# Turning the layer-0 feed-forward's quads and the layer-1 attention's pairs by block transposes and two row transfers in place of TensorE transposes

## Chip, cores and metric

One NeuronCore of a Trainium2 chip runs the whole program. The metric is the device time of one execution in microseconds (us), the median of several runs. All data are 32-bit floats.

## What is computed

A two-layer vision tower over 32 images of 3 x 256 x 256. Each image becomes 256 tokens of 256 features. The reference, cut to the order of the work and to the two places that the change touches:

```python
h = tokenizer(x)                                   # 32 x 256 x 256
h = h + L0_attn(layernorm(h))                      # gated attention, relu squared
h = h + L0_ffn(layernorm(h))
h = h + L1_attn(layernorm(h))
h = h + L1_ffn(layernorm(h))                       # experts in 4 heads

# L0_ffn: the 127 best of the 256 tokens of an image go through the layer, the others get x alone
weights = x @ wr + br
sel = x[top 127 tokens by weights]
y = (gelu(sel @ w1 + b1) @ w2 + b2) * weights[sel]
out = zeros.at[sel].set(y) + x

# L1_attn: phases from two small networks, a causal memory over the tokens
key   = tanh(gelu(x @ Wk1 + bk1) @ Wk2 + bk2) * freq * pi
query = tanh(gelu(x @ Wq1 + bq1) @ Wq2 + bq2) * freq * pi
retrieved = real(sum(cumsum(exp(i key) * (x @ Wv + bv)) * exp(-i query))) / sqrt(position * K)
out = x + layernorm(retrieved) @ Wo + bo
```

Here `x` is the layer-normed input of each layer. `sel @ w1` and `x @ Wk1`, `x @ Wq1` sum over features, so on TensorE the features of `sel` and `x` must lie along the partitions; they are made with tokens along the partitions. Turning them round is what the change is about.

## The kernel before, in words

The program is written as five stages. A (tokenizer), B (layer-0 attention), C (layer-0 feed-forward), D (layer-1 attention) are recorded by hand: each engine executes its instructions in the order in which the Python code issues them, and waits are put in where data or buffers need them. E (layer-1 feed-forward) is ordered by a table. The images' states `H[b]` (128 partitions x 2 x 256, token `c * 128 + p` in partition `p`) stay on the chip throughout. All matmuls are recorded at line 116, in the helper `mm`; PSUM has eight banks, taken in turn (`bank`).

**Turning tokens to features** is done in two ways. On TensorE, `transposed` (L180 to 190) and `turn_c` (L225 to 231) transpose 128x128 tiles against an identity into two PSUM banks, and `copy_split` (L192 to 196) copies the first bank by ScalarE (L194), the second by VectorE (L196). Stage B has another way for 14 of its 16 pairs: `blocks_b` (L262 to 271) transposes 32x32 blocks on VectorE into `b_blocks`, and four DMAs write them to a DRAM buffer, `turned_b` (L273 to 277) reads them back by four more DMAs. All DMAs named here are issued by SyncE's queue (SP) in order; SP waits at an issue until what it needs is there.

**Stage B** handles a pair of images a step, t from 0 to 17. In each step it also normalises the following pair (`norm_b`, `blocks_b`). From t = 4 on it ranks the tokens of finished images for stage C: `rank_c` scatters an image's tokens to the DRAM buffer `ranked` by their rank, and `first_ranks` (L220 to 223) loads the first 128 ranks of four images, a quad, into `cs`. At t = 17 `turn_c` turns quad 0, between `gated_b` and `output_b`.

**Stage C** has eight quads, four steps to a quad. `ORDER_C` (L877) says what runs at which step of quad u (step 0 is t = 4u): hidden_c at 0 and 1 (`sel @ w1`, two halves of 16 matmul records each), made at 2 and 3 (`@ w2`, two images each, results written to DRAM by SP at L850), `turn_c` at -1, first_ranks at -8, fetch at 4 and 5 (gathers by GpSimd), update at 5 and 6 (VectorE: `H` updated at L869 and its statistics at L124). In a step the entries are issued in the order of the list, so `turn_c` of the next quad stands between the two `made`. At t = 30, the last but one, `norm_d` normalises the first two pairs of stage D into `cx`.

**Stage D** has 16 pairs of images, three steps of t to a pair. For pair u, `do(k, f)` runs f at t = 3u + k:

- 0: norm_d (L809 to 822) writes the pair's normalised tokens `dx` (four buffers, two per pair)
- 1: turn (L911 to 913), the transposes into `dxT`; residual_d on GpSimd
- 2: hidden, two networks of two 128-wide parts each, and Gelu on ScalarE
- 3: phases: small matmuls, Tanh, then L943, L946, L947 on VectorE, then Sin on ScalarE into `dz`
- 4: match: matmuls of `dz` with itself; VectorE multiplies by the causal mask into `dat` (L963)
- 5: memory: matmuls of `dat` and `dx`, copied to `dm` by ScalarE (L976)
- 6: output: matmuls of `dm` and `wvo` into four banks, statistics by VectorE (L987, L988)
- 7: add_output adds the four banks to `H` (L997) and so frees them; stats_e

Steps of different pairs with the same t are interleaved: at t = 3u + 2 stand hidden of pair u and memory of pair u - 1, at t = 3u + 3 phases of u, output of u - 1 and norm_d of u + 1, at t = 3u + 4 the transposes of u + 1, add_output of u - 1 and match of u. The first pairs differ: pair 1 is turned at t = 2. At t = 6, 9 and 12 the last entries of `ORDER_C` follow, fetches and updates of the last quad.

Of the kernel before, what the change touches and what calls it, by code (L numbers as in the profile page):

```python
# [80 lines left out]
def vit_tower(tc, a, out):  # L81
# [15 lines left out]
    def bank():  # L97
        return ppool.tile([P, 512], F32, name="bank", tag="bank")
# [81 lines left out]
    def transposed(xT, xs, copy):  # L180
# [3 lines left out]
        for k in range(2):  # L184
# [4 lines left out]
                    nc.tensor.transpose(p[:, o : o + P], x[:, c, k * P : (k + 1) * P], ident)  # L189
            copy(k, xT[:, k, :], p[:, 0:w])  # L190

    def copy_split(k, o, i):  # L192
        if k == 0:
            nc.scalar.copy(o, i)  # L194
        else:
            nc.vector.tensor_copy(o, i)  # L196
# [25 lines left out]
        for j in range(4):  # L222
            nc.sync.dma_start(s.x[:, j, :], ranked[b0 + j][0:P, :])

    def turn_c(b0, s, _):  # L225
        s.xsel = p0.tile([P, 2, 4 * P], F32, name="xsel")
        for k in range(2):
            p = bank()
            for j in range(4):
                nc.tensor.transpose(p[:, j * P : (j + 1) * P], s.x[:, j, k * P : (k + 1) * P], ident)  # L230
            copy_split(k, s.xsel[:, k, :], p)

    wpool = region.enter_context(tc.tile_pool(name="w_c", bufs=1))
    region_b = ExitStack()
# [26 lines left out]

    def blocks_b(b0, s):  # L262
        s.d = pdram.tile([32, 16 * NC, 4, 32], F32, name="b_turned", bufs=2)
        y = px.tile([P, 8, 2 * NC, 32], F32, name="b_blocks", bufs=1)
        for j, x in enumerate(s.xs):
            nc.vector.transpose(
                y[:, :, j * NC : (j + 1) * NC, :].rearrange("p f c t -> p c f t"),
                x.rearrange("p c (f t) -> p c f t", t=32),
            )
        for i in range(4):  # L270
            nc.sync.dma_start(s.d[:, :, i, :], y[32 * i : 32 * i + 32].rearrange("p f c t -> p (f c) t"))
# [150 lines left out]
    with (  # L422
# [96 lines left out]
        for t in range(B // 2 + 2):  # L519
            new, old, older, next_one = pair(t) if t else None, pair(t - 1), pair(t - 2), pair(t + 1)  # L520
            next_one = next_one if t else None
            if t == 1:
                turn_b(*new, p2, "bxT")
            if t >= 4:
                turned = turn_weights(2 * (t - 4))
            if old:
                scores_b(*old)
            if new:
                base_b(*new, p2.tile([P, 2 * N], F32, name="base"))
            if t >= 4:  # L530
                ranks(2 * (t - 4), turned)
                if t in (5, 7):
                    first_ranks(2 * t - 10, quads[t // 2 - 2], 0)
            if new:
                queries_b(*new, p2.tile([P, 2 * N], F32, name="bq"), p2.tile([P, 2 * N], F32, name="bk"))
            if old:
                gates_b(*old)
            if t == 1:
                factors_b(*powers)
            if next_one:  # L540
                norm_b(*next_one)
                blocks_b(*next_one)
            if old and t >= 3:
                norms_c(2 * (t - 3))
            if old:
                values_b(*old)
            if next_one:
                bias_b(*next_one)
            if old and t >= 3:
                residuals_c(2 * (t - 3))  # L550
            if next_one:
                turned_b(*next_one, p2, "bxT")
            if older:
                gated_b(*older)
                if t == B // 2 + 1:
                    turn_c(0, quads[0], 0)
                    norms_c(2 * (t - 3))
                    residuals_c(2 * (t - 3))
                output_b(*older)
# [249 lines left out]
    def norm_d(b0, s, pool, name, bufs):  # L809
        s.xs = []  # L810
        for j in range(2):
# [10 lines left out]
                )  # L822
            s.xs.append(x)

    def residual_d(b0, s):
        for j in range(2):
            h = H[b0 + j]
            nc.gpsimd.tensor_tensor(h, h, s.xs[j], ALU.add)
            nc.gpsimd.tensor_tensor(h, h, over(add_row, [P, NC, D], 1), ALU.add)

    with region_c:
        st_d = new_stats("d")

        def hidden_c(b0, s, half):
            if half == 0:
                s.hT = p2.tile([P, 8, 4 * P], F32, name="hT")
            for m in range(4 * half, 4 * half + 4):
                p = bank()
                for k in range(2):
                    mm(p, w1[:, k, m * P : (m + 1) * P], s.xsel[:, k, :], k == 0, k == 1)  # L840
                nc.scalar.activation(s.hT[:, m, :], p, AF.Gelu_apprx_tanh, bias=col("b1", m))

        def made(b0, s, half):
            for j in range(2 * half, 2 * half + 2):
                p = bank()
                for m in range(8):
                    mm(p[:, 0:D], s.hT[:, m, j * P : (j + 1) * P], w2[:, m, :], m == 0, m == 7)
                y = p2.tile([P, D], F32, name="cy", bufs=4)
                nc.vector.tensor_tensor(y, p[:, 0:D], row_c("b2"), ALU.add)
                nc.sync.dma_start(results[b0 + j][:], y)  # L850

        def fetch(b0, s, half):
            s.y = s.y if half else []
            for b in range(b0 + 2 * half, b0 + 2 * half + 2):
                y = px.tile([P, NC, D], F32, name="cx", bufs=8)
                for c in range(NC):
                    k = b * NC + c
                    nc.gpsimd.indirect_dma_start(
                        y[:, c, :], None, results[b][:], bass.IndirectOffsetOnAxis(rank_of[:, k : k + 1], 0)
                    )  # L860
                s.y.append(y)

        def update(b0, s, half):
            for j in range(2 * half, 2 * half + 2):
                b = b0 + j
                st, rs, i = at(st_d, b)
                for c in range(NC):
                    k = b * NC + c
                    nc.vector.scalar_tensor_tensor(  # L869
                        H[b][:, c, :], s.y[j][:, c, :], w_kept[:, k : k + 1], H[b][:, c, :], ALU.mult, ALU.add  # L870
                    )
                    stats(st, i, c, H[b][:, c, :])
            pow_rstd_of(st_d, b0 + 2 * half, 2)

        ORDER_C = ((0, hidden_c, 0), (1, hidden_c, 1), (2, made, 0), (-1, turn_c, 0), (-8, first_ranks, 0),  # L877
                   (3, made, 1), (4, fetch, 0), (5, fetch, 1), (5, update, 0), (6, update, 1))

        def step_c(t):  # L880
            for at_step, do, j in ORDER_C:
                u, r = divmod(t - at_step, 4)
                if r == 0 and 0 <= u < B // 4 and (u > 1 or do is not first_ranks):
                    do(4 * u, quads[u], j)

        END_C = 4 * (B // 4 - 1) + 4
        pairs = [Pair() for _ in range(B // 2)]
        preparing = prepare()
        for t in range(END_C):
            if t == 0:  # L890
                norms_c(B - 2)
                residuals_c(B - 2)
            if t == END_C - 2:
                for u in range(2):
                    norm_d(2 * u, pairs[u], px, "cx", 8)
            step_c(t)
            if t < 2:
                ranks(B - 4 + 2 * t, turn_weights(B - 4 + 2 * t))
            if t >= 8:
                next(preparing, None)  # L900
        passing.close()
# [5 lines left out]
    with (  # L907
        tc.tile_pool(name="d_2", bufs=2, reuse_waits="tile") as p2,
        tc.tile_pool(name="d_8", bufs=8, reuse_waits="tile") as p8,
    ):  # L910
        def turn(b0, s):  # L911
            s.xT = p2.tile([P, 2, 2 * N], F32, name="dxT")
            transposed(s.xT, s.xs, copy_split)

        def hidden(b0, s, i, ms=(0, 1)):

# [3 lines left out]
            for m in ms:  # L920
                p = bank()
                for k in range(2):
                    mm(p, (wk1, wq1)[i][:, k, m * P : (m + 1) * P], s.xT[:, k, :], k == 0, k == 1)
                nc.scalar.activation(g[:, m, :], p, AF.Gelu, bias=bias_d[:, 2 * i + m : 2 * i + m + 1])

        def phases(b0, s):
# [81 lines left out]
        for t in range(3 * (NP - 1) + 8):  # L1008
# [3 lines left out]
                    which(2 * u, pairs[u], *more)  # L1012

            last = t == 3 * NP + 1
            if t != 4:
                do(1, turn)
            if not last:
                do(7, add_output)
            if t != 4:
# [7 lines left out]
            do(2, hidden, 0)  # L1027
            if t == 2:
                do(2, hidden, 1)
                turn(2, pairs[1])  # L1030
            elif t == 5:
                do(2, hidden, 1, (0,))
                match(0, pairs[0])
# [4 lines left out]
            do(3, phases)  # L1038
            if t == 5:
                residual_d(2, pairs[1])  # L1040
            if t > 3:
                do(0, norm_d, p8, "dx", 4)
            if t == 3 * NP:
                output(B - 4, pairs[NP - 2], (0, 1, 2))
            else:
# [740 lines left out]
def _layout(i):  # L1786


    def blocks(w, p=P):
        k, m = w.shape[0] // p, w.shape[1]  # L1790
        return w.reshape(k, p, m).transpose(1, 0, 2)

    def column(v, p=P):
        return v.reshape(-1, p).T

# [29 lines left out]
    def pairs(w):  # L1825
# [12 lines left out]
        "rows_e": np.concatenate([rows_e[n] for n in ROWS_E]),  # L1838
        "wuv": blocks(i["L0_attn_W_uv"]),
        "wo": blocks(i["L0_attn_W_o"]),  # L1840
        "w1": blocks(i["L0_ffn_w1"]),
        "w2": blocks(i["L0_ffn_w2"]),
        "before": before,
        "wk1": blocks(i["L1_attn_Wk1"]),
        "wq1": blocks(i["L1_attn_Wq1"]),
        "wk2": blocks(twice(i["L1_attn_Wk2"])),
        "wq2": blocks(twice(i["L1_attn_Wq2"])),
        "wv1": blocks(i["L1_attn_Wv"]),
# [40 lines left out]
```

## Time and profile before

| what | us |
|---|---|
| median of three runs | 1913.17 (1910.04 to 1913.69) |
| the profiled execution's own time | 1911.49 |
| its span | 1909.7 |
| TensorE busy | 1864.9 |
| VectorE busy | 1313.2 |
| ScalarE busy | 805.8 |
| GpSimd busy | 757.6 |

In the profile, PE is TensorE, PEld its weight loads, DVE VectorE, ACT ScalarE, POOL GpSimd, SP SyncE; L is a line of the kernel. The page gives each engine's busy time and share, then 40 equal slices of the span (digits are tenths), then DMA queues, then the chain: from the last instruction back, at each step to what released it, as shares of the span. A timeline row is start, length, engine, line, operation, tiles written <- read, shapes, count, and in brackets the idle time before it with what ended it. Durations of matmuls overlap, since they are pipelined: one 128x512 record lasts 592 ns, but the next starts 0.43 us after it. PEclk is the share of full speed that the clock of TensorE was granted; in this execution it was 1.00 nearly everywhere, 0.94 and 0.98 in the stretches from 180 and 200 us, 0.84 in that from 1000 us, and lower at the very end. A DMA row gives the number of issues, the size of each and the median time from issue to landing. In the page's list of DMA issues cs<-ranked has 3.5 us for 128 KB.

Stage C's first hidden matmul is at 681.7 us and its last matmul before D's transposes ends at 918 us; D's first transposes are at 917.96 and stage E's work begins at about 1260 us.

### The profile page before, as it was taken

The numbers are of one execution on the slowest core, as the hardware profiler recorded it, in microseconds if no ns is written. First come the engines' busy times: TensorE is split into PE (matmuls) and PEld (weight loads), VectorE is DVE, ScalarE is ACT, GpSimd is POOL, SyncE is SP. The second block draws the span as 40 slices with busy tenths as digits, with TensorE's granted clock in tenths as the row PEclk, the third lists the DMA queues.
The fourth block names the chain that finished last, engine by engine and source line by source line (L and its number), as shares of the span: only waits on it lengthen the run. The fifth ranks groups of instructions, "written<-read, shape, count | busy, mean of one in ns | idle before, by whom it ended". The sixth has DMA issues, their size and how long they took to land.

```text
span 1909.7 us, 36912 instructions
## 1 busy us (share of the span) xinstructions
PE 1864.9 (98%) x14740; PEld 1323.7 (69%) x14740; DVE 1313.2 (69%) x3271; ACT 805.8 (42%) x1632; POOL 757.6 (40%) x792
## 2 busy tenths in 40 slices
PE   9999999999999999999989999999999999999993
PEld 8887566666676776766645555567888878787872
DVE  2335478787878563534465555544999999999998
ACT  0001222121212112122334444447787888888772
POOL 1224233333434253424343433324454545555553
PEclk9999999999999999999999999999999999999995
DMA  9550121212121042212000000001222222222211
GB/s 312 151 156 18 35 61 46 71 42 58 47 54 44 34 136 63 82 54 61 15 20 1 1 1 0 1 18 24 58 52 62 58 57 63 52 63 53 64 44 57
DMA packets 132226, 109.17 MB, mean 57 GB/s; under 512 B 67792, under 2 KB 110288, under 8 KB 131664
## 3 DMA queue, kind: packets, MB, share of 16 engines
q1 hardware_dynamic: 125328, 89.17, 17.4%
q0 software_dynamic: 6144, 16.79, 2.8%
q8 instruction: 118, 1.93, 0.4%
q10 hardware_dynamic: 576, 0.79, 0.1%
q14 instruction: 60, 0.49, 0.1%
HBM read 53.75 MB, written 28.31 MB: 43 GB/s over the span
## 4 chain that ended last, share of the span: by engine, by line
PE 94%; DVE 4%; issue 1%; ACT 0%; DMA 0%; SPq 0%; POOL 0%; DVEq 0%; ACTq 0%
PE bank L116 91%; PE bank L792 2%; PE bank L189 1%; PE bank L230 0%; PE bank L500 0%; DVE six L124 0%; DVE fout L1387 0%; DVE fout L1401 0%; DVE eo L1265 0%; DMA b_turned<-b_blocks 0%; DVE ranges L1288 0%; DVE six L987 0%; DVE fout L1390 0%; DMA bxT<-b_turned 0%; DVE h L869 0%
## 5 line engine op out<-in xcount | busy, mean ns | idle before, releaser
L1184 POOL TENSOR_SCALAR_AFFINE_SELECT et<-et 128x512 f32<-128x512 f32 (+1 forms) x192 | 166.2, 878 | 201.6 <-ACT et L1175 199.7
L1175 ACT ACTIVATE et<-bank 128x512 f32<-128x512 f32 x384 | 207.7, 630 | 30.7 <-PE bank L116 30.2
L116 PE MATMUL bank<-ev,et 128*64 128x68 f32 (+1 forms) x6144 | 198.9, 225 | 0.0
L116 PEld LDWEIGHTS bank<-ev,et 128*64 128x64 f32 x6144 | 191.5, 137 | 5.7 <-issue 4.7
L116 PE MATMUL bank<-g,sx 64*128 64x512 f32 (+1 forms) x512 | 177.6, 486 | 0.0
L116 PE MATMUL bank<-g,sw 64*128 64x512 f32 (+1 forms) x512 | 177.2, 486 | 0.0
L116 PE MATMUL bank<-tokW,patch 128*128 128x256 f32 x768 | 167.6, 381 | 0.0
L116 PEld LDWEIGHTS bank<-tokW,patch 128*128 128x128 f32 x768 | 146.6, 191 | 21.4 <-DMA tokW<-in_tokW_dram 0.7
L116 PE MATMUL bank<-bxT,w_wuv 128*128 128x512 f32 x300 | 133.0, 598 | 2.5 <-DMA bxT<-b_turned 2.5
L1204 ACT COPY eo<-bank 128x280 f32<-128x280 f32 x256 | 96.0, 396 | 68.3 <-PE bank L116 61.6
L116 PEld LDWEIGHTS bank<-g,sx 64*128 64x128 f32 x512 | 93.1, 187 | 31.6 <-issue 22.7
L116 PE MATMUL bank<-wvo,dm 128*128 128x512 f32 x256 | 114.3, 599 | 0.0
L116 PE MATMUL bank<-attn,bv 128*128 128x256 f32 x512 | 113.1, 379 | 0.0
L116 PE MATMUL bank<-w_wo,gT 128*128 128x256 f32 x512 | 113.1, 379 | 0.0
L116 PE MATMUL bank<-w_w,hT 128*128 128x256 f32 x512 | 113.1, 379 | 0.0
L116 PE MATMUL bank<-xsel,w_w 128*128 128x512 f32 x256 | 111.4, 593 | 0.0
L116 PEld LDWEIGHTS bank<-attn,bv 128*128 128x128 f32 x512 | 97.2, 190 | 19.6 <-issue 7.2
L124 DVE BATCH_NORM_STATS2 six<-h 128x6 f32<-128x256 f32 x256 | 105.5, 412 | 4.4
L116 PEld LDWEIGHTS bank<-w_w,hT 128*128 128x128 f32 x512 | 96.6, 190 | 15.3 <-issue 2.9
L116 PEld LDWEIGHTS bank<-g,sw 64*128 64x128 f32 x512 | 93.1, 187 | 20.1 <-issue 9.9
L116 PEld LDWEIGHTS bank<-w_wo,gT 128*128 128x128 f32 x512 | 97.2, 190 | 13.2
L116 PE MATMUL bank<-w_wuv,bxT 128*128 128x512 f32 x240 | 105.4, 592 | 0.0
(276 smaller groups left out, 3712.6 us busy)
## 6 DMA issues: line engine op xcount, KB each, us to landing
patch<-in_patches_dram SPq DMA_DIRECT2D x31, 768.0 KB, 4.6
sw<-sx SPq DMA_DIRECT2D x64, 128.0 KB, 2.3
out_dram<-fout SPq DMA_DIRECT2D x32, 256.0 KB, 2.4
both<-fxT SPq DMA_DIRECT2D x62, 128.0 KB, 2.4
both<-hx SPq DMA_DIRECT2D x62, 128.0 KB, 2.3
b_turned<-b_blocks SPq DMA_DIRECT2D x56, 128.0 KB, 3.3
bxT<-b_turned SPq DMA_DIRECT2D x56, 128.0 KB, 3.1
cs<-ranked SPq DMA_DIRECT2D x32, 128.0 KB, 3.5
```

What stands on the lines that cost most here:

```text
L116: nc.tensor.matmul(o, lhsT, rhs, start=first, stop=last)
L124: nc.vector.bn_stats(six, x)
L189: nc.tensor.transpose(p[:, o : o + P], x[:, c, k * P : (k + 1) * P], ident)
L792: nc.tensor.transpose(p[:, o : o + P], x[:, c, k * P : (k + 1) * P], ident)
L1175: nc.scalar.activation(t2[:, i, :], p, AF.Exp)
L1184: nc.gpsimd.affine_select(out=own, in_=own, pattern=[[0, 2 * n_e], [1, P]], compare_op=ALU.is_ge, fill=0.0, base=0, channel_multiplier=-1,)
L1204: nc.scalar.copy(im.o[:, g * OC : (g + 1) * OC], p[:, 0:OC])
```

## The change

Quads of C and pairs of D are turned as stage B's pairs were, but by larger transfers: VectorE transposes 32x32 blocks (one instruction for a quad, two for a pair), one DMA writes the result to DRAM in rows of 4 KB, one DMA reads it back in pieces of 1 KB. The features come back in another order, four groups of 32 partitions interleaved, so `w1`, `wk1`, `wq1` are laid out by the host in that order (`turned`), and hidden's moving operand `s.f[:, k]` is read with three dimensions, in runs of 32 elements. The transposes at TensorE and the copies that followed them are gone from C and D; pairs 0 and 1 of B keep theirs.

The placing: in C `blocks_c` runs at step -3 and `moved_c`, the read, at step -2, where `turn_c` was at -1. Quad 0 is done at t = 15 of B. For D's pairs 0 and 1 the blocks and the write stand at t = 30 of C, behind norm_d, into free `cs` buffers; the reads are issued at t = 1 and 2 of D. For pairs from 2 on, norm_d moves from step 0 to step -1, and the blocks, write and read follow it there. `blocks` in B and C is one shared buffer; `dxB` in D is one buffer; the DRAM buffer `c_turned` has two.

```diff
+    def blocks_turned(y, xs, d):
+        y5 = y.rearrange("p (f s t) -> p s f t", f=4, t=32)
+        n = 8 // len(xs)
+        for j, x in enumerate(xs):
+            nc.vector.transpose(
+                y5[:, j * n : (j + 1) * n], x.rearrange("p c (k f t) -> p (c k) f t", k=2, f=4)
+            )
+        nc.sync.dma_start(d.rearrange("i q x -> (i q) x"), y)
+
+    def moved(xT, d):
+        nc.sync.dma_start(xT, d.rearrange("i q (f x) -> (q f) i x", f=4))
+        return xT.rearrange("p i (s k t) -> p k s i t", k=2, t=32)
...
-    def turn_c(b0, s, _):
-        s.xsel = p0.tile([P, 2, 4 * P], F32, name="xsel")
...
+    def blocks_c(b0, s, _):
+        s.d = pdram.tile([4, 32, 4 * N], F32, name="c_turned", bufs=2)
+        blocks_turned(px.tile([P, 4 * N], F32, name="blocks", bufs=1), [s.x], s.d)
+
+    def moved_c(b0, s, _):
+        s.f = moved(p0.tile([P, 4, 2 * P], F32, name="xsel"), s.d)
...
+            if t == B // 2 - 1:
+                blocks_c(0, quads[0], 0)
+                moved_c(0, quads[0], 0)
             if older:
                 gated_b(*older)
                 if t == B // 2 + 1:
-                    turn_c(0, quads[0], 0)
...
+    def blocks_d(b0, s, pool, name, shape, bufs):
+        y = pool.tile(shape, F32, name=name, bufs=bufs)
+        s.d = pdram.tile([4, 32, 4 * N], F32, name="c_turned", bufs=2)
+        blocks_turned(y.rearrange("p j d -> p (j d)"), s.xs, s.d)
...
-                    mm(p, w1[:, k, m * P : (m + 1) * P], s.xsel[:, k, :], k == 0, k == 1)
+                    mm(p, w1[:, k, m * P : (m + 1) * P], s.f[:, k], k == 0, k == 1)
...
-        ORDER_C = ((0, hidden_c, 0), (1, hidden_c, 1), (2, made, 0), (-1, turn_c, 0), (-8, first_ranks, 0),
+        ORDER_C = ((0, hidden_c, 0), (1, hidden_c, 1), (2, made, 0), (-3, blocks_c, 0), (-2, moved_c, 0), (-8, first_ranks, 0),
...
             if t == END_C - 2:
                 for u in range(2):
                     norm_d(2 * u, pairs[u], px, "cx", 8)
+                for u in range(2):
+                    blocks_d(2 * u, pairs[u], p0, "cs", [P, 4, D], 2)
...
-        def turn(b0, s):
-            s.xT = p2.tile([P, 2, 2 * N], F32, name="dxT")
-            transposed(s.xT, s.xs, copy_split)
+        def moved_d(b0, s):
+            s.f = moved(p2.tile([P, 4, N], F32, name="dxT"), s.d)
...
-                    mm(p, (wk1, wq1)[i][:, k, m * P : (m + 1) * P], s.xT[:, k, :], k == 0, k == 1)
+                    mm(p, (wk1, wq1)[i][:, k, m * P : (m + 1) * P], s.f[:, k], k == 0, k == 1)
...
-            if t != 4:
-                do(1, turn)
+            if t == 1:
+                do(1, moved_d)
...
             if t == 2:
                 do(2, hidden, 1)
-                turn(2, pairs[1])
+                moved_d(2, pairs[1])
...
-            if t > 3:
-                do(0, norm_d, p8, "dx", 4)
+            if t > 4:
+                do(-1, norm_d, p8, "dx", 4)
+                do(-1, blocks_d, p8, "dxB", [P, 2 * NC, D], 1)
+                do(-1, moved_d)
...
+    def turned(w):
+        w = blocks(w)
+        return w.reshape(4, 32, *w.shape[1:]).swapaxes(0, 1).reshape(w.shape)
...
-        "w1": blocks(i["L0_ffn_w1"]),
+        "w1": turned(i["L0_ffn_w1"]),
...
-        "wk1": blocks(i["L1_attn_Wk1"]),
-        "wq1": blocks(i["L1_attn_Wq1"]),
+        "wk1": turned(i["L1_attn_Wk1"]),
+        "wq1": turned(i["L1_attn_Wq1"]),
```

More of the change, by code (lines that the diff above doesn't have):

```diff
@@ L223, in first_ranks @@
             nc.sync.dma_start(s.x[:, j, :], ranked[b0 + j][0:P, :])
-    def turn_c(b0, s, _):
-        s.xsel = p0.tile([P, 2, 4 * P], F32, name="xsel")
[L227 to L231, printed above, removed]
+    def blocks_c(b0, s, _):
[3 more added lines that the diff above has]
+        s.f = moved(p0.tile([P, 4, 2 * P], F32, name="xsel"), s.d)
     wpool = region.enter_context(tc.tile_pool(name="w_c", bufs=1))
@@ L263, in blocks_b @@
         s.d = pdram.tile([32, 16 * NC, 4, 32], F32, name="b_turned", bufs=2)
-        y = px.tile([P, 8, 2 * NC, 32], F32, name="b_blocks", bufs=1)
+        y = px.tile([P, 4 * N], F32, name="blocks", bufs=1)
+        y = y.rearrange("p (f c t) -> p f c t", f=8, t=32)
         for j, x in enumerate(s.xs):
```

## The prediction, made before the changed kernel ran

> **What bounds the kernel now.** I read the page first: engines, slices, chain.
>
> ```profile
> PE 1864.9 (98%) x14740; PEld 1323.7 (69%) x14740; DVE 1313.2 (69%) x3271; ACT 805.8 (42%) x1632; POOL 757.6 (40%) x792
> ...
> PE   9999999999999999999989999999999999999993
> ...
> PE 94%; DVE 4%; issue 1%; ACT 0%; DMA 0%; SPq 0%; POOL 0%; DVEq 0%; ACTq 0%
> ```
>
> TensorE is the bound almost everywhere: 94% of the chain is matmuls. So a matmul taken away is worth its place in TensorE's queue, if nothing else then comes late. Two stages are touched: layer-0 feed-forward (C, about 675 to 918 us) and layer-1 attention (D, about 919 to 1260 us). Of D I read the timeline of one pair (start, length, engine, line, tiles):
>
> ```profile
> 1105.14 1.04 PE L189 MATMUL bank<-ident,dx 128*128 128x128 f32 x8
> ...
> 1106.11 1.58 PE L116 MATMUL bank<-dz 64*128 64x256 f32 x16
> ...
> 1107.62 3.70 PE L116 MATMUL bank<-dxT,w_wk 128*128 128x512 f32 x8
> ...
> 1114.59 2.78 PE L116 MATMUL bank<-dat,dx 128*128 128x256 f32 x16
> ...
> 1117.40 0.58 ACT L976 COPY dm<-bank 128x512 f32<-128x512 f32 x1 [0.72 <-PE bank L116]
> ```
>
> Each group begins where the one before ends: the pair's transposes, match, hidden, memory, then phases and output. The transposes recur at 1084.14, 1105.14, 1126.15: a pair takes 21.0 us. Two pairs take longer (23.7 and 26.9 us, from 970.5, 994.2 and 1021.1). There TensorE waits:
>
> ```profile
> 975.83 0.66 DVE L196 COPY dxT<-bank 128x512 f32<-128x512 f32 x1
> ...
> 976.54 2.84 PE L116 MATMUL bank<-dxT,w_wk 128*128 128x512 f32 x6 [2.44 <-DVE dxT L196]
> ```
>
> ```profile
> 1000.45 5.49 PE L116 MATMUL bank<-dxT,w_wk 128*128 128x512 f32 x6 [2.64 <-DVE dxT L196]
> ```
>
> VectorE is busy with the last images' updates (L869, L124), and its half of the transpose's copy stands behind them. After the second wait the matmuls run at half speed: the clock granted in 1000 to 1020 us was 0.84, 3.2 us lost. The two waits and the dip are the 2.7 + 5.9 us by which these periods exceed 21.0.
>
> **Removed.** 64 transposes at L230 (8 quads) and 128 at L189 (16 pairs; 16 of L189's 144 belong to B and stay). Their row says 273 ns each, and the Trainium skill ("TensorE: Matmul & The Clock Gate", Part 4: PE-mode transpose) has about 275 ns in a kernel's context; by that 192 of them are 52 us. But the durations overlap: in the timeline eight start at 1105.14 and the next group at 1106.11, 0.97 us; in C eight start at 703.17 and the next matmul at 704.04, 0.87 us. I take the starts: C 8 x 0.87 = 7.0 us, D 0.97 us for each pair but pair 0 (below), 15 x 0.97 = 14.6 us. Also removed: the copies (ACT 585 ns, DVE 658 to 680 ns per quad or pair), off the path except in the two waits.
>
> The two waits go: hidden then needs a transfer made a period before, and not the late VectorE copy. What is late next: hidden's third group takes a PSUM bank that add_output (L997) frees, after the same updates. In the 994 us pair the updates cannot end before about 999.2 (output's last matmuls end at 994.2, one bn_stats, 4.2 us of updates), add_output frees a bank at 999.65; hidden, begun at 995.7, reaches that group at 999.2. About 0.5 us of wait remains in each, and dat (to 1001.8) is in time for memory at 1002.7. So 2.7 + 5.9 - 1.0 = 7.6 us gained; other end 0, if the updates hold something else as long.
>
> **Added on VectorE.** Block transposes: the nearest row is stage B's,
>
> ```profile
> L266 DVE STREAM_TRANSPOSE b_blocks<-cx x28: 661/685/707, 185.1 to 584.6; 128x512 f32<-128x512 f32 x28
> ```
>
> so 2 x 0.69 us per pair, and about 1.2 us for a quad's single 128x1024. VectorE is at 11 to 12 of 20 us in D and at 5 to 12 in most of C: hidden, nothing. Those of pairs 0 and 1 (2.7 us) follow norm_d at 903.1, where VectorE has nothing until 908.0. Quad 0's stands in the step of B that has no next pair to normalise, so less VectorE work than the steps before.
>
> norm_d and the blocks move one step earlier and now wait: dx has four buffers, so pair u's tiles are pair u-2's, which memory (L116, `dat,dx`) reads last in that same step. Queued behind them on VectorE are the phases' three operations (L943, L946, L947), first at 1120.23. By the ACT copies of dm, memory's halves are read by 1116.1 and 1117.4; norm_d takes 2 x 1.1 us (1102.01 to 1104.24), the blocks 1.4: done at 1119.7, before 1120.2. If this ends 0.5 us late, Sin still has 2 us before match.
>
> **Added transfers, and the new loop.** SP issues 512 KB out and 512 KB back, 1 KB or more a packet. For D this decides:
>
> ```profile
> patch<-in_patches_dram SPq DMA_DIRECT2D x31, 768.0 KB, 4.6
> ...
> out_dram<-fout SPq DMA_DIRECT2D x32, 256.0 KB, 2.4
> ...
> b_turned<-b_blocks SPq DMA_DIRECT2D x56, 128.0 KB, 3.3
> bxT<-b_turned SPq DMA_DIRECT2D x56, 128.0 KB, 3.1
> ...
> results<-cy SPq DMA_DIRECT2D x32, 128.0 KB, 1.7
> ```
>
> Writes: 1.7 us for 128 KB, 2.4 for 256; my estimate for 512 in rows of 4 KB is 3.0. Reads: 768 KB in 4.6 us, w_wk's 256 KB in 2.9; estimate between them 3.7. With 0.4 us of hand-overs 7.1 us. Lower end 5.6 (out's and w_wk's own times, 0.3 between); upper end stage B's round trip of the same 512 KB in eight pieces, first issue 186.45, TensorE released 197.72: 11.3 us. I take 7.1: packet size and issue are like patch's, not like b_turned's (67,792 packets under 512 B).
>
> Available: hidden of the next pair begins one period after 1107.62, without the transposes at 1127.65; from 1119.7 that is 7.95 us. So it just fits, with 0.85 us to spare, and the period becomes 20.03 us. In C there is more room: moved_c's read is issued after made 0's second result (911.92 in the last quad) and hidden follows at 918: 6 us for 3.7, and the write went a step before.
>
> On SP's queue the quad's write stands ahead of results' writes and the read between them; the read waits for the write landed and for hidden's last matmul, both past by then. results' two later writes are not held.
>
> **The start of D is worse.** Pair 0's read is queued on SP behind the four results of the last quad. The last is issued at 918.83 (0.32 us), so the read goes at about 919.3 and lands at 922.85; before, hidden began at 919.45. Lost: 3.4 us, less if the read is as quick as w_wk's (2.9). TensorE, done at 917.96, is idle 4.9 us. The nearest row for what follows is the dip after the 2.64 us wait, 3.2 us (after a 2.5 us wait at 195 us: clock 0.94 and 0.98, 1.6 us; after the 2.44 us one: none). The skill's same page ("Why this matters for your kernels") warns of idle gaps over about 3 us, with windows of about 3.4 us; one window at half rate is 1.7 us. I take 3.4 us, since this gap is longer than any of those; the other end is 0. Pair 1's read follows at once and has 7 us of hidden before it is needed.
>
> **Matmuls on a strided operand.** Hidden's 256 + 256 records now read the moving side in runs of 32 elements. No row has this; the contiguous ones start every 0.43 us and those in two runs of 128 (g,sw) keep 376 ns for 256 columns like contiguous ones (379). I take no change; other end 5% of 220 us, 11 us. A gain is excluded: the same columns are streamed.
>
> **Sum** against the profiled execution, 1911.49 us (span 1909.7; the three runs have a median of 1913.17): -7.0 - 14.6 - 7.6 + 3.4 + 3.4 = -22.4, so 1889 us.
>
> **Rivals.**
> (A) Slower: D becomes a loop through memory. Memory's end, norm_d, blocks, write, read, hidden, memory: 12.1 us (1107.62 to 1119.7) plus the round trip. Beyond 7.95 us each us costs 14 pairs x 1 us. At B's 11.3 us the pair takes 23.4, +47 us: 1936, without further clock dips. It is slower than before from a round trip of 9.55 us (22.4/14 above 7.95). For it: stage B's transfers really take so long, and HBM is read just after it is written. Against: those are 128 B packets and four issues of 0.6 us; D has almost no other traffic (1 GB/s). Chance 0.10, 0.07 of it slower.
> (B) The transposes go, but the two waits stay, at add_output or dat: 22.4 - 7.6 = 14.8, 1897 us. For: VectorE's updates are unmoved. Against: norm_d's 2.2 us leave that step. Chance 0.16.
> (C) Runs of 32 slow the matmuls by 5%: 1900 us. Chance 0.05; slower than before from 10%, 0.01.
> The likeliest, 1889 (1882 to 1896): 0.69.
>
> The range 1881 to 1902 takes in B, C, and a start of D without a dip (1886) and a bit less; A is left out. Changes under 0.2% cannot be told from none here. Faster by more 0.89, within 0.03 (A and C near their thresholds), slower 0.08 (A 0.07, C 0.01).
>
> **What would show it.** Right: no L189 rows with dx and no L230; hidden starting right behind match in D, period 20.0 us; transfers c_turned 3.0 and read 3.7; no wait on dxT by DVE near 976 and 1000; a TensorE gap of 4 to 5 us before D's first hidden, with the clock below 1 after it. Wrong: hidden in D waiting for a DMA in every pair (A); waits of 2 us on L997 or dat in the two pairs (B); hidden's pitch above 0.43 us (C).

## The result and the profile after

The changed kernel takes 1898.07 us (median of four runs, 1897.41 to 1899.32); the kernel before, run beside it, 1912.42 us (median of four, 1910.04 to 1913.69). The ratio is 0.9925, with a 95% interval of 0.9912 to 0.9938: faster by 14 us, where 24 were predicted (1889 against 1913; 22.4 in the sum). The profiled executions differ by as much: 1911.49 us before, 1897.49 after, with spans of 1909.7 and 1895.8.

The page of the changed kernel: TensorE's and the other engines' busy time, its busy tenths in 40 slices, its clock in the same slices, and the chain by engine.

```profile
PE 1845.8 (97%) x14548; PEld 1305.8 (69%) x14548; DVE 1350.6 (71%) x3287; ACT 792.0 (42%) x1608; POOL 758.1 (40%) x792
...
PE   9999999999999999999899999999999999999993
...
PEclk9999999999999999999999999999999999999995
...
PE 92%; DVE 4%; DMA 2%; issue 1%; ACT 0%; SPq 0%; POOL 0%; DVEq 0%
```

All 192 transposes of C and D are gone (14740 records before, 14548 after). TensorE is still the bound, but DMA now has 2% of the chain where it had 0%. Marks on TensorE's timeline cut the span into stretches, and say where the time went:

| stretch | before | after | difference | predicted |
|---|---|---|---|---|
| start to C's first hidden | 681.65 | 681.69 | 0.0 | -0.9 |
| C: first hidden to the last record of made | 236.31 | 230.23 | -6.1 | -6.1 |
| start of D: to the first phases | 9.43 | 14.66 | +5.2 | +5.8 |
| D: first phases to the last record of memory | 329.00 | 314.15 | -14.85 | -21.2 |
| E: to the last record of `ev,et` | 607.19 | 608.81 | +1.6 | 0 |
| from there to the end of the span | 46.13 | 46.25 | +0.1 | 0 |
| sum | 1909.71 | 1895.79 | -13.9 | -22.4 |

(The predicted column is the sum of the prediction cut at the same marks: quad 0 of C stands in the first stretch, pair 1's transposes in the third.) The gain falls short of the sum by 8.5 us, and most of that, 6.3 us, is in the steady part of D. Its timeline after the change, hidden of three pairs and match of the last (start, length, engine, line, tiles, count, and in brackets the idle time before it and what ended it):

```profile
1033.81 3.70 PE L116 MATMUL bank<-dxT,w_wk 128*128 128x512 f32 x8
...
1054.55 1.96 PE L116 MATMUL bank<-dxT,w_wk 128*128 128x512 f32 x4 [0.54 <-DMA dxT<-c_turned]
```

```profile
1073.15 1.58 PE L116 MATMUL bank<-dz 64*128 64x256 f32 x16
1074.65 3.70 PE L116 MATMUL bank<-dxT,w_wk 128*128 128x512 f32 x8
```

The last pair is as predicted: hidden right behind match, and 20.1 us after the pair before (1054.55 to 1074.65). The pair at 1054.55 comes 20.74 us after the one before, with a wait of 0.54 us on the read, and every second pair has such a wait, 0.54 to 0.60 us: at 1054.55, 1095.45, 1136.30, 1177.15 and 1218.02. Around the last updates of C the same wait is 0.53 us (991.67) and 1.22 us (1013.71). The clock is full here, and what TensorE waits for is the read: it comes late.

The start of D, in the same view:

```profile
912.33 0.42 DVE L870 TENSOR_TENSOR cy<-bank,rows_c 128x256 f32<-128x256 f32 x1 [1.95 <-PE bank L116]
...
912.78 0.32 SPq L871 DMA_DIRECT2D results<-cy  x1
913.21 0.98 SPq L203 DMA_DIRECT2D dxT<-c_turned  x2
...
917.26 5.95 PE L116 MATMUL bank<-dxT,w_wk 128*128 128x512 f32 x8 [4.96 <-DMA dxT<-c_turned]
```

The reads of pairs 0 and 1 are issued right behind the last result, and TensorE waits 4.96 us. Its first eight records then last 5.95 us, not 3.70: the granted clock was half from 915.0 to 921.8 us.

**Are the transfers to blame?** The list of DMA issues (KB each, median us to landing):

```profile
dxT<-c_turned SPq DMA_DIRECT2D x16, 512.0 KB, 3.8
...
c_turned<-dxB SPq DMA_DIRECT2D x14, 512.0 KB, 2.6
```

Estimated were 3.7 and 3.0. From the write's issue (1047.91) to hidden (1054.55) it is 6.64 us; 7.1 were put down, and 7.95 were thought available. So the round trip was quicker than predicted and still too late, and what failed lies ahead of it. The write was issued 14.1 us after the hidden ahead of it began (1033.81 to 1047.91), where the prediction had 12.1.

VectorE's and GpSimd's rows between memory and the write in that pair, and the write:

```profile
1040.55 1.27 POOL L849 TENSOR_TENSOR h<-h,dx 128x512 f32<-128x512 f32 x1
...
1041.90 1.27 POOL L850 TENSOR_TENSOR h<-h,add_row 128x512 f32<-128x512 f32 x1
...
1042.29 2.31 DVE L835 TENSOR_SCALAR dx<-h,rs_d,d_one 128x256 f32<-128x256 f32 x2 [2.85 <-PE bank L116]
1043.12 1.32 POOL L849 TENSOR_TENSOR h<-h,dx 128x512 f32<-128x512 f32 x1
...
1044.52 1.27 POOL L850 TENSOR_TENSOR h<-h,add_row 128x512 f32<-128x512 f32 x1
1044.70 1.13 DVE L833 TENSOR_SCALAR d_one<-d_one 128x2 f32<-128x2 f32 x1
...
1045.93 0.73 DVE L835 TENSOR_SCALAR dx<-h,rs_d,d_one 128x256 f32<-128x256 f32 x2
1046.59 1.30 DVE L197 STREAM_TRANSPOSE dxB<-dx 128x512 f32<-128x512 f32 x2
...
1047.91 0.33 SPq L200 DMA_DIRECT2D c_turned<-dxB  x1
```

Two norm_d instructions take 0.73 us once GpSimd is quiet, 2.31 us beside it. A two-element instruction (L833) takes 1.13 us and ends at 1045.83, when GpSimd's last addition ends (1045.79). GpSimd is at residual_d, which the change didn't touch: norm_d was moved to where it runs. From memory's first half to the end of the blocks it is 5.6 us instead of 3.6.

The theory to be tested is then: GpSimd's residual_d stretches norm_d on VectorE, and that makes D's loop through memory late by half a microsecond in every second pair. The rivals: the round trip or SP's queue is what is late; norm_d is slow for another reason. For the start of D the theory is the place of the read in SP's queue; the rival, that something else is next to be late.

### The profile page after: what moved, and what is told of

It is laid out like the page before. It is cut to its first block, busy times and chain, and to the rows that moved or that the text cites. A ratio compares the mean times of both kernels' runs of the same rounds, so it can differ in the third digit from the quotient of the medians.

```text
span 1895.8 us, 36643 instructions
## 1 busy us (share of the span) xinstructions
PE 1845.8 (97%) x14548; PEld 1305.8 (69%) x14548; DVE 1350.6 (71%) x3287; ACT 792.0 (42%) x1608; POOL 758.1 (40%) x792
## 4 chain that ended last, share of the span: by engine, by line
PE 92%; DVE 4%; DMA 2%; issue 1%; ACT 0%; SPq 0%; POOL 0%; DVEq 0%
PE bank L116 90%; PE bank L808 2%; DMA dxT<-c_turned 2%; PE bank L514 0%; DMA patch<-in_patches_dram 0%; DVE fout L1411 0%; DVE fout L1425 0%; DVE dx L835 0%; DVE eo L1289 0%; DVE six L124 0%; DMA b_turned<-blocks 0%; DMA bxT<-b_turned 0%; DVE ranges L1312 0%; DVE fout L1414 0%; DVE ey L1374 0%
## 5 line engine op out<-in xcount | busy, mean ns | idle before, releaser
L862 ACT ACTIVATE hT<-bank,cols 128x512 f32<-128x512 f32 x64 | 44.0, 687 | 186.7 <-PE bank L116 186.7
L124 DVE BATCH_NORM_STATS2 six<-h 128x6 f32<-128x256 f32 x256 | 105.5, 412 | 4.4
L116 PEld LDWEIGHTS bank<-w_w,hT 128*128 128x128 f32 x512 | 97.1, 190 | 15.4 <-issue 2.9
```

What stands on the lines that cost most here:

```text
L116: nc.tensor.matmul(o, lhsT, rhs, start=first, stop=last)
L124: nc.vector.bn_stats(six, x)
```

## Experiments

Each kernel was made from the changed one; "ratio" is against the kernel before, with its 95% interval. The changed kernel's own is 0.9925. The medians of the kernel before in the two series were 1913.36 and 1912.72 us.

**1. Six `dx` buffers**, so that norm_d needn't wait for memory.

```diff
-                do(-1, norm_d, p8, "dx", 4)
+                do(-1, norm_d, p8, "dx", 6)
```

> The changed kernel with six dx buffers instead of four: norm_d no longer waits for memory of the pair two before, so VectorE's part of the loop (norm_d, block transposes, write) leaves the path. Theory (loop through memory, lengthened because norm_d runs beside GpSimd's residual_d): the waits of 0.54 to 0.59 us on the read in every second pair of D and the larger ones near 992 and 1014 us go, every pair takes 20.1 us, 4 to 5 us less: 1893 to 1894 us, although single norm_d instructions may still be stretched beside GpSimd. Rival (the round trip through DRAM or SP's queue is what is late): the waits on the read stay, 1898 us.

Measured: 1892.03 us, ratio 0.9886 (0.9869 to 0.9902). D's stretch takes 309.18 us instead of 314.15, the steady pairs 20.13, and no wait on the read is left. norm_d is stretched even more, two instructions in 2.76 us:

```profile
1039.15 0.76 DVE L835 TENSOR_SCALAR dx<-h,rs_d,d_one 128x256 f32<-128x256 f32 x2
...
1040.22 2.76 DVE L835 TENSOR_SCALAR dx<-h,rs_d,d_one 128x256 f32<-128x256 f32 x2
1040.23 1.27 POOL L849 TENSOR_TENSOR h<-h,dx 128x512 f32<-128x512 f32 x1
...
1042.91 1.29 DVE L197 STREAM_TRANSPOSE dxB<-dx 128x512 f32<-128x512 f32 x2
```

It starts at 1039.15, ahead of memory, whose first weights are loaded at 1040.03, and not behind memory's first half; so the stretching is hidden. The rival that the round trip or SP's queue is what is late falls: the same transfers are in time when they start earlier.

**2. residual_d ahead of stats_e.** The four buffers, and with them the loop, stay.

```diff
+            if t != 4:
+                do(1, residual_d)
             do(7, stats_e)
-            if t != 4:
-                do(1, residual_d)
```

> The changed kernel with residual_d issued ahead of stats_e in its step, so that GpSimd adds while VectorE is at add_output, dat and statistics, and is done about 1 us earlier than norm_d can start; dx keeps four buffers and the loop through memory stays. Theory (GpSimd's additions stretch norm_d): two norm_d instructions of 256 columns take 0.73 us again instead of 2.31, first half of memory read to end of blocks 3.6 us instead of 5 to 5.6, waits on the read in the steady pairs gone: 3 to 4.5 us less, 1894 to 1895. Rival (norm_d is slow by itself, or the loop would be late with any VectorE time): 1898, waits unchanged. A cost could be that the statistics of VectorE are stretched instead; then add_output or dat would be late and the gain smaller.

Measured: 1892.81 us, ratio 0.9893 (0.9877 to 0.9910); D's stretch 309.17 us. The timeline of a pair:

```profile
1037.32 1.27 POOL L850 TENSOR_TENSOR h<-h,add_row 128x512 f32<-128x512 f32 x1
...
1038.09 0.51 DVE L832 SCALAR_TENSOR_TENSOR d_one<-st_d,rs_d 128x2 f32<-128x2 f32 x1
...
1041.28 0.73 DVE L835 TENSOR_SCALAR dx<-h,rs_d,d_one 128x256 f32<-128x256 f32 x2 [2.47 <-PE bank L116]
...
1043.24 1.30 DVE L197 STREAM_TRANSPOSE dxB<-dx 128x512 f32<-128x512 f32 x2
```

GpSimd is done at 1038.59; norm_d waits for memory (PE) as it should and takes 0.73 us; from memory's first half to the end of the blocks it is 3.3 us. The cost that was feared didn't come: beside GpSimd's additions the statistics (L124) keep 403 ns and add_output 476 ns, as before. What was stretched here is a single small one, L832, 0.51 us, to the end of GpSimd's instruction. Around the last updates of C the collision is not quite gone: five norm_d instructions before 1003 us still last 0.95 to 1.36 us, and hidden waits 0.22 us for its read at 992.33.

**3. No residual_d at all**: its two calls in D are taken out.

> The changed kernel without GpSimd's residual_d in D (so the images' states lack the layer's input and its added row; this part of the computation is left out). It isolates the collision. Theory: no norm_d instruction of 256 columns longer than 0.45 us, the waits on the read in steady pairs gone, about 1893 to 1895 us. Rival (the collision is not with these additions): long norm_d instructions and waits of 0.5 us remain, 1898 us.

Measured: 1891.42 us, ratio 0.9883 (0.9867 to 0.9900); D's stretch 309.17 us, the same as in the two experiments above. The instructions of norm_d's line (ns, minimum, median and maximum), in the changed kernel

```profile
L835 DVE TENSOR_SCALAR dx<-h,rs_d,d_one x56: 404/413/1434, 936.7 to 1209.7; 128x256 f32<-128x256 f32 x56
```

and in this one

```profile
L835 DVE TENSOR_SCALAR dx<-h,rs_d,d_one x56: 405/410/415, 939.5 to 1205.8; 128x256 f32<-128x256 f32 x56
```

Without residual_d none is long. Experiments 2 and 3 remove the collision in two ways, experiment 1 takes norm_d off the path and leaves the collision; all three gain the same 5.0 us in D. So much does the collision with residual_d cost.

**4. Pair 0's read in the last step of C**, into the free `blocks` buffer.

```diff
+            if t == END_C - 1:
+                pairs[0].f = moved(
+                    px.tile([P, 4 * N], F32, name="blocks", bufs=1).rearrange("p (i x) -> p i x", i=4), pairs[0].d
+                )
             step_c(t)
...
-            if t == 1:
-                do(1, moved_d)
```

> The changed kernel with the read for D's pair 0 issued in the last step of C ahead of the last quad's results, into a buffer that is free then, instead of behind them. Theory (the 5.0 us that TensorE waits at D's start and the half-speed window after it come from that read's place on SP's queue): hidden of pair 0 starts within 0.3 us of the end of C's matmuls, no window of half clock near 915 to 922 us, 6.5 to 7.5 us less: about 1891 us. Rival (pair 1's read or VectorE is next to be late, or a half-speed window comes anyway): 3 to 5 us less, 1893 to 1895 us.

Measured: 1889.37 us, ratio 0.9878 (0.9862 to 0.9895). The start of D, TensorE:

```profile
912.69 3.60 PE L116 MATMUL bank<-blocks,w_wk 128*128 128x512 f32 x8
...
916.12 3.60 PE L116 MATMUL bank<-blocks,w_wq 128*128 128x512 f32 x8
```

Hidden stands right behind made, the eight records take 3.60 us, and no half-speed window is there. The stretch takes 7.18 us instead of 14.66, 7.5 us less. In D's steady part the waits of 0.5 us in every second pair stay (1047.63, 1088.49 and on), as they should: this is another cause.

**5. C's half alone.** `blocks_c` and `moved_c` as changed; `turn` and norm_d at step 0 in D.

> Stage C's half of the change alone: the quads turned by block transposes and transfers, D's pairs by TensorE as before, wk1 and wq1 laid out as before. Theory: the eight quads' transposes are worth 0.87 us each and nothing else comes late, D is as before with its two waits on the copy: 7 us less than before, about 1906 us. Rival (most of the whole gain of 14 us is C's, because in D the waits ate it): 10 us or more less.

Measured: 1906.25 us, ratio 0.9969 (0.9956 to 0.9981), 6.5 us less by the medians. C's stretch is 230.23 us as in the whole change: 6.08 us for seven quads, 0.87 each. D keeps its two long waits on the copy, 2.44 and 2.56 us. Its stretch is yet 1.4 us shorter than before, 327.62 us: half clock was granted for 3.41 us after the first of them (971.95 to 975.36), where the kernel before had 6.83 us at the second (999.69 to 1006.52).

**6. D's half alone.** `turn_c` and its place in `ORDER_C` as before.

> Stage D's half of the change alone, C's quads turned by TensorE as before. Theory: the whole change saves 14.0 us in the profiled pair and 7.0 of them are C's, so D's half saves about 7 to 8.5 us net (13 for 15 pairs' transposes at 0.87 us, 8.6 for the two long waits and the slow clock, less 6 to 7 for the start of D and 6 for the waits on the read): about 1905 us. Rival (the halves help each other through VectorE or SP's queue): the two halves do not add up to the whole, off by more than 2 us.

Measured: 1903.81 us, ratio 0.9956 (0.9942 to 0.9969), 8.9 us less. The halves add up to 15.4 us, the whole has 14.3: no more apart than the intervals allow. The stretches say it better: start of D 14.84 us and D 314.27, as in the whole change (14.66 and 314.15), and C 236.31, as before.

**7. norm_d and what follows it at step 0**, where norm_d stood before.

```diff
-            if t > 4:
-                do(-1, norm_d, p8, "dx", 4)
-                do(-1, blocks_d, p8, "dxB", [P, 2 * NC, D], 1)
-                do(-1, moved_d)
+            if t > 3:
+                do(0, norm_d, p8, "dx", 4)
+                do(0, blocks_d, p8, "dxB", [P, 2 * NC, D], 1)
+                do(0, moved_d)
```

> The changed kernel with norm_d, the blocks, the write and the read of D's pairs at step 0 (where norm_d stood before the change) instead of one step earlier. Theory (the lead of one step is what hides the round trip): VectorE comes to norm_d only after the phases of the pair ahead, blocks end about when hidden should start, so each pair from 2 on waits for nearly a whole round trip, 5 to 7 us with half-speed windows in places: 70 to 110 us more than the changed kernel, 1970 to 2010 us, slower than before. Rival (the transfers need no lead, since VectorE and SP run ahead): within 5 us of the changed kernel.

Measured: 1991.67 us, ratio 1.0415 (1.0396 to 1.0434): slower. One pair:

```profile
1056.05 0.74 DVE L835 TENSOR_SCALAR dx<-h,rs_d,d_one 128x256 f32<-128x256 f32 x2
...
1057.82 1.30 DVE L197 STREAM_TRANSPOSE dxB<-dx 128x512 f32<-128x512 f32 x2
...
1059.15 0.33 SPq L200 DMA_DIRECT2D c_turned<-dxB  x1
...
1062.28 0.36 SPq L203 DMA_DIRECT2D dxT<-c_turned  x1
...
1066.01 2.90 PE L116 MATMUL bank<-dxT,w_wk 128*128 128x512 f32 x3 [5.61 <-DMA dxT<-c_turned]
```

norm_d isn't stretched here (0.74 us), yet most of the round trip is on the path: 5.0 to 5.6 us of waiting in each pair. A pair takes 27.1 to 27.7 us, on average 7.2 more than 20.13. The 1.7 to 2.0 us beyond the wait are the clock: a half-speed window of 6.83 us came in every pair from 2 on (at 1035.31, 1062.61, 1089.92 and so on), and hidden's first eight records take 5.4 to 5.7 us instead of 3.70. The round trip is on TensorE's path here as rival A feared, but not by A's loop: norm_d stands behind the phases' operations on VectorE (the last, L969, ends at 1055.67) and doesn't wait for memory. The move by one step is what makes the transfers cheap.

**8. Both mends**, experiments 2 and 4 together.

> The changed kernel with both mends: residual_d ahead of stats_e, and pair 0's read ahead of the last quad's results into a free buffer. Theory: the two causes are independent, the gains measured alone (about 5 us in D's pairs, 7 us at D's start) add up: 1884 to 1885 us, no wait over 0.3 us before hidden. Rival (they share a cause, or the half-speed window moves into D): 1888 to 1890 us.

Measured: 1884.20 us, ratio 0.9853 (0.9838 to 0.9868), the fastest of all. In its timeline

```profile
1021.88 1.58 PE L116 MATMUL bank<-dz 64*128 64x256 f32 x16
1023.39 3.70 PE L116 MATMUL bank<-dxT,w_wk 128*128 128x512 f32 x8
1026.93 3.60 PE L116 MATMUL bank<-dxT,w_wq 128*128 128x512 f32 x8
```

no row before hidden has brackets. Start of D 7.18 us and D 309.16: the two gains, 7.5 and 5.0 us, add up. They are 12.5 us in these two stretches; by the medians, which come from different series, the kernel is 13.9 us faster than the changed one.

## Why the prediction was right in its mechanism and off in its size

The sign and the mechanism hold: transposes gone, transfers hidden, two long waits gone, a worse start of D. The sum was 8.5 us too large, roughly 5.0 for a collision that it put at nothing, 1.5 for the transposes of D, 0.9 in the first stretch and 1.6 in E that are differences between executions, less 0.6 at the start of D. Step by step:

- **C, 8 x 0.87 us: right.** Seven quads in C's stretch measure 6.08 us. A quad's block transpose takes 1.24 us where 1.2 was put. The transfers were slower than put, 3.5 to 5.9 us for a write and 3.9 to 4.3 for a read of the quads within C where 3.0 and 3.7 stand, but no row of hidden in C waits for its read: the lead of two steps hid it. Quad 0's share is in the first stretch, where the kernel's start came 0.8 us later in the profile after (first matmul of `bq` and `bk` at 194.16 against 193.34). Between the profiles of all these kernels that mark lies anywhere from 193.3 to 198.5 us, with the same code ahead of it. From the mark to C's first hidden it is 488.3 and 488.4 us in the two kernels that turn quad 0 by TensorE (before, experiment 6) and 487.4 to 487.7 in the six others that have a half-speed window near 200 us as these two have, so about the 0.87 us that was put.
- **D's transposes, 15 x 0.97 us: each is worth 0.87.** Free pairs take 20.13 us, not 20.03. The 0.97 us were the distance from the transposes to match. But from output's start it was 6.97 us to the transposes (1098.17 to 1105.14), and it is 7.07 to match (1066.08 to 1073.15): a tenth stays. 1.5 us in all.
- **The two waits on VectorE's copy and the dip, 7.6 us: right.** Without the collision D takes 309.17 us, 19.83 less than before; 14 x 0.87 = 12.2 of it are transposes, which leaves 7.6. Part of this is luck: the dip of 3.2 us after the second wait belongs to the execution that was profiled, and in experiment 5 the same two waits cost 1.4 us less. The rest wait was put at 0.5 us each on a bank freed by add_output; there is one of 0.27 us.
- **The start of D, +3.4 and +3.4: nearly right.** Hidden began 5.3 us after the last record of made where it began 1.5 us after it before, 3.85 us more; then it took 9.31 us (917.26 to 926.57) instead of 6.97 (919.45 to 927.39, less 0.97 for pair 1's transposes), 2.3 more. The reads of pairs 0 and 1 were issued together and landed after 4.0 and 4.9 us; the prediction had 3.6. A window that began after 2.7 us of waiting and lasted 6.83 us, twice the 3.4 us of the prediction, cost less than its 3.4, since a third of it fell on the wait. (The Trainium skill's page that the prediction names gives the window's 3.4 us in its Part 1, "What's actually happening"; the section named has the idle gap alone.)
- **The failed step: "norm_d takes 2 x 1.1 us (1102.01 to 1104.24), the blocks 1.4: done at 1119.7".** The durations are from a place where GpSimd was idle, and norm_d was moved away from it. Memory's first half to the end of the blocks took 2.0 us more in the pair shown (5.6 instead of 3.6), so the "0.85 us to spare" became a lack of 0.54, though the round trip was 0.46 us quicker than put. The phases' operations stand behind norm_d on VectorE, as the prediction says, and there is room for this in all pairs but one: at 1010.91 match waits 0.58 us for Sin (rows below), after norm_d and the blocks had lasted from 1000.12 to 1007.01. The loop then closes at 20.13 + 0.6 us in every second pair. Why only there is read from the timeline, and not tried by itself: GpSimd's start hangs on stats_e and so on output, which stands ahead of the wait. When hidden has waited, memory comes later and GpSimd's additions don't, so norm_d meets less of them; from memory's first half to the end of the blocks it was 5.6 us in one pair and 5.0 in the next. The cost is 5.0 us by three experiments.
- **E, 1.6 us, not predicted, and nothing ties it to the change.** The profile after has a window of half clock at 1816.12 to 1819.53 us which that of before hasn't. In all ten profiles TensorE has a gap of 2.07 to 2.09 us at this place of E; in three of them such a window follows (the changed kernel, 6 at 1827.78, 8 at 1801.89), in seven none, six of them kernels with the change or a half of it.

The rows of the pair whose match waits:

```profile
1000.12 1.76 DVE L835 TENSOR_SCALAR dx<-h,rs_d,d_one 128x256 f32<-128x256 f32 x2 [0.77 <-PE bank L116]
...
1005.72 1.29 DVE L197 STREAM_TRANSPOSE dxB<-dx 128x512 f32<-128x512 f32 x2
...
1010.91 1.58 PE L116 MATMUL bank<-dz 64*128 64x256 f32 x16 [0.58 <-ACT dz L970]
```

The rest of the rivals: A's loop is what bound, but with a round trip of 6.6 us and a longer VectorE part; its price, one us per pair for each us late, was too low where TensorE waits long enough for half-speed windows (experiment 7: about 7.2 us for a wait of 5.3). B is out: the two waits are gone. That the measured 1898 us lies beside B's 1897 is chance, the sum of other misses. C is out: hidden's eight records with a full clock take 3.60 to 3.70 us, as before, and start every 0.43 us; runs of 32 elements cost nothing.

**It could have been seen before.** The timeline of the kernel before, at the place that norm_d was to move to:

```profile
1092.95 1.26 POOL L828 TENSOR_TENSOR h<-h,dx 128x512 f32<-128x512 f32 x1
1093.58 2.78 PE L116 MATMUL bank<-dat,dx 128*128 128x256 f32 x16
...
1094.29 1.27 POOL L829 TENSOR_TENSOR h<-h,add_row 128x512 f32<-128x512 f32 x1
1095.09 0.58 ACT L976 COPY dm<-bank 128x512 f32<-128x512 f32 x1 [0.62 <-PE bank L116]
1095.52 1.27 POOL L828 TENSOR_TENSOR h<-h,dx 128x512 f32<-128x512 f32 x1
...
1096.86 1.28 POOL L829 TENSOR_TENSOR h<-h,add_row 128x512 f32<-128x512 f32 x1
```

Memory's first half is read at 1095.09, so norm_d would start there, and GpSimd adds until 1098.14. And the same operation in the same shape, in stage B, beside GpSimd's work (minimum, median and maximum in ns):

```profile
L175 DVE TENSOR_SCALAR cx<-h,st_b,rs_b x64: 401/407/1358, 147.7 to 583.7; 128x256 f32<-128x256 f32 x64
```

The median agrees with norm_d's 411, but the maximum is 1358, near what norm_d showed later (1434). The long ones lie beside GpSimd's L256: one runs from 148.65 to 150.01 us, GpSimd's from 148.50 to 149.86. The Trainium skill ("SBUF — State Buffer", section "SBUF: two separate sides") says that VectorE and GpSimd share a pair of ports that one of them holds for a whole instruction while the other blocks, for some kinds of VectorE operation and not for others. That fits what was measured: waits up to the end of GpSimd's instruction, for tensor_scalar from SBUF to SBUF. From it and these rows an estimate could have been made: up to 1.27 us for each of GpSimd's instructions that norm_d meets. Of the four of residual_d, three end after norm_d could start, and 0.85 us was to spare.

## What to carry to other kernels

When an instruction is moved, take its duration from the place it goes to: look at what the other engines do there, GpSimd next to VectorE above all, and read the maximum of a group and not only its median. When transfers replace work on the bounding engine, what counts is the lead: the same round trip of 6.6 us cost nothing with a step's lead and a free VectorE, 0.54 us in every second pair with a stretched one, and 7 us in each pair without the lead. The first transfer of a stage has no period ahead of it; put its issue ahead of what else is in its queue.

## What the runs showed that was not expected

- VectorE beside GpSimd: a tensor_scalar of 128x256 from SBUF takes up to 1.43 us instead of 0.41, one of 128x2 1.13 instead of 0.17. In the kernel before, one of 128x256 at L175 lasted 4.4 us (304.16 to 308.54, the second of the two in the timeline below). It began while GpSimd issued an indirect DMA (303.69 to 304.65) and lasted until the last of three GpSimd instructions that followed each other closely had ended at 308.38; six of this group's 64 are like it. Others were let in between: norm_d's at 1042.29 ended at 1043.31, when one GpSimd instruction had ended (1043.16) and the next had begun (1043.12). What decides this isn't shown. Block transposes (experiment 1: 1.29 us for two, as ever), statistics (experiment 2: 403 ns) and add_output from PSUM (476 ns) beside the same GpSimd instructions keep their times.

```profile
L175 DVE TENSOR_SCALAR cx<-h,st_c,rs_c x64: 365/406/4385, 238.3 to 688.6; 128x256 f32<-128x256 f32 x64
```

```profile
303.84 4.70 DVE L175 TENSOR_SCALAR cx<-h,st_c,rs_c 128x256 f32<-128x256 f32 x2
304.67 2.49 POOL L256 TENSOR_TENSOR h<-h,rows_b 128x512 f32<-128x512 f32 x2
307.11 1.27 POOL L400 TENSOR_TENSOR h<-h,cx 128x512 f32<-128x512 f32 x1
```

- A wait of about 5.3 us on TensorE cost 7.2, since half of the clock was granted for 6.83 us, beginning 2.2 us after the wait had begun in experiment 7 (1062.61), 2.7 us in the changed kernel (915.0). All 20 waits of 4.9 to 5.6 us in these profiles have such a window. Waits of 0.5 to 1.3 us in D have none. After the gaps in between, 2.07 to 2.66 us, half clock came in some executions and not in others: in three of ten in E, in eight of ten near 200 us in B, after two of the four waits on VectorE's copy in D. The 3 us that the prediction cites are so no bound here.
- 512 KB in rows of 4 KB to DRAM landed, in D, in 2.6 us (one in 4.5) and came back in 3.5 to 3.9 us, quicker than the same amount in eight pieces in stage B (11.3 us from first issue to TensorE). In C the same two transfers took 3.5 to 5.9 and 3.9 to 4.3 us, together 7.5 to 10.2 us. Four of the seven are above the 7.95 us that the prediction had for D: a transfer's duration, too, hangs on the place it is taken from.
